# A gather-paced recommendation kernel: VectorE operations with two SBUF inputs replaced by operations that read PSUM

## The chip, the cores and the metric

One core of one Trainium2 chip. The metric is the device time of one launch, in microseconds. Several runs are made and their median is given. The cores of this chip have four compute engines that matter here: TensorE (matmuls, PE in the profile), VectorE (DVE), ScalarE (ACT) and GpSimd (POOL). GpSimd issues the indirect DMAs that gather rows of an embedding table.

## The reference, cut to what matters

For each of 16384 users, 69 rows of 96 floats are looked up (`u`), and one row for the label (`q`). A small net gives each looked-up row an attention weight, the weighted rows are summed in 10 groups, and a top net of three layers gives one number per user.

```python
u = emb[batch_user]                       # 16384 x 69 x 96
z = concat([q, u, q - u, q * u])
h = dice(z @ W1 + b1, a1)                 # dice(x) = (alpha*(1-p) + p)*x, p = sigmoid(x)
att = (h @ W2 + b2) @ W3 + b3
pre = where(batch_user < ITEM_NUM, u * att, 0)
pooled = einsum('gf,bfe->bge', window, pre)
x = concat([pooled, ql])
h = dice(bn(x @ Wf1 + bf1), af1)
h = dice(bn(h @ Wf2 + bf2), af2)
return h @ Wf3 + bf3
```

Here `ql` is the label's row, and `q` is that row repeated for each of the user's 69. An id equal to ITEM_NUM must give a zero row, although the table has a row of its own there.

## The kernel before: the parts that the change and the argument touch

The kernel works in 1104 steps. In each step GpSimd gathers 8 times 128 rows, one indirect DMA each, and TensorE turns the rows of that step, computes the hidden layer of an earlier one, and pools the rows of one that lies eight steps back. With 128 gathers for the labels there are 8960 gathers.

```python
def map_ids(n, ids):                      # ids that mean "no row" move to a zero row at the table's end
    rows = ipool.tile([P, NT], I32, tag="rows", name=f"rows{n}")
    nc.vector.scalar_tensor_tensor(rows, ids[:, 0:NT], float(ITEM_NUM), ids[:, 0:NT], ALU.is_ge, ALU.add)
    return rows
...
def gather(dst, index):                   # 128 rows, one index per partition
    nc.gpsimd.indirect_dma_start(out=dst, out_offset=None, in_=emb,
        in_offset=bass.IndirectOffsetOnAxis(ap=index, axis=0))
...
def hidden(i, ph, uT, quT):
    ...
    nc.vector.tensor_mul(y, ph, y)        # one input in PSUM, one in SBUF
...
def spread(b, row):                       # once in 4 steps
    pt = ps_x.tile([P, 4, 4, 32], F32, tag="x", name=f"patt{b}")
    for t in range(4):
        nc.tensor.transpose(pt[:, t]..., row[:, t * P : (t + 1) * P], ident)
    nc.vector.tensor_scalar(w, pt[:, :, :, 0:2]..., bb, None, ALU.add)
    nc.vector.tensor_tensor(rw..., R...to_broadcast(...), w...to_broadcast(...), ALU.mult)   # both in SBUF
    return rw
...
# top net, each half of the first layer (and the second layer likewise)
nc.vector.tensor_scalar(x1, p1, S_BN, sbf1[h], ALU.mult, ALU.add)
nc.scalar.activation(g1, x1, AF.Sigmoid, scale=S_DICE)
nc.scalar.activation(g1, g1, AF.Identity, bias=af1c[h], scale=naf1c[h])
nc.vector.tensor_mul(x1, x1, g1)          # both in SBUF
```

## Time and profile before

| | kernel before |
|---|---|
| time, unprofiled, first three runs | 11350.36 us (11344.71 to 11351.59) |
| span of the profiled execution | 13499.4 us |
| GpSimd busy / gathers | 8525.6 us / 8960 |
| TensorE busy, granted clock | 10109.4 us, 0.658 |
| VectorE busy | 3172.4 us |

The two times differ by 2149 us, and a reader has to decide which of them the profile explains. The prediction does that from the gathers, and shows the lines. A row of the groups reads: line, engine, operation, output <- inputs, shapes, count | busy us in all, mean ns of one | idle us just before it, and what ended that idle time.

### The profile page before, as it was taken

Reading aid. Unit: us, or ns where it says so; the run is one execution under the profiler, and the core shown is the slowest. Engines: PE = TensorE matmul, PEld = TensorE weight load, DVE = VectorE, ACT = ScalarE, POOL = GpSimd, SP = SyncE. Lnnn points to the kernel's source line nnn. Section 1 sums busy time; section 2 is a strip of 40 time slices with the busy share of each in tenths; the row PEclk is TensorE's granted clock in tenths of the full one; section 3 lists DMA queues with packets and bytes.
Section 4 is the critical chain, followed back from the end, with each engine's and each line's share of the span. In section 5 each row is a group of like instructions: output and inputs, shape, how many; then the busy total and the mean of one; then the engine's idle time right before and its main releaser. Section 6 shows DMA issues by size and latency. Waiting matters only on the chain.

```text
span 13499.4 us, 108113 instructions
## 1 busy us (share of the span) xinstructions
PE 10109.4 (75%) x41348; PEld 5068.4 (38%) x41348; DVE 3172.4 (24%) x5424; ACT 3740.6 (28%) x6086; POOL 8525.6 (63%) x8966
## 2 busy tenths in 40 slices
PE   4777777778777776777777777777778777787778
PEld 2333333334333333333333333333333333343334
DVE  2222222222222222222222222222222222222222
ACT  1222222223222222222222222222222222232222
POOL 6666666666666666666666666666666666666664
PEclk5666666666666677666666666766666666666657
DMA  1111111111111111111111111111111111111111
GB/s 37 34 34 35 33 34 33 34 35 34 34 34 34 34 34 33 33 34 34 33 34 34 34 34 35 34 33 33 33 35 34 34 33 34 35 34 33 34 32 22
DMA packets 295008, 453.59 MB, mean 34 GB/s; under 512 B 145952, under 2 KB 151104, under 8 KB 294496
## 3 DMA queue, kind: packets, MB, share of 16 engines
q0 software_dynamic: 286720, 440.98, 15.5%
q8 instruction: 331, 5.42, 0.2%
q1 hardware_dynamic: 6142, 4.77, 0.1%
q14 instruction: 181, 1.48, 0.0%
q10 hardware_dynamic: 1634, 0.94, 0.0%
HBM read 446.04 MB, written 0.07 MB: 33 GB/s over the span
## 4 chain that ended last, share of the span: by engine, by line
PE 62%; another core or an unknown queue 15%; issue 12%; ACT 5%; DVE 5%; POOL 1%; DMA 0%; DVEq 0%; POOLq 0%; ACTq 0%
PE ph L326 22%; PE acc L376 15%; PE ptr L308 9%; PE p L406 5%; PE prow L337 4%; PE ph L278 4%; DVE y L330 3%; ACT y L329 2%; PE patt L353 2%; ACT y L328 1%; PE pa L346 1%; DVE quT L311 1%; ACT uT L319 1%; POOL u L227 1%
## 5 line engine op out<-in xcount | busy, mean ns | idle before, releaser
L227 POOL DMA_INDIRECT u<-in_emb,rows x8832 | 8401.6, 951 | 4802.4 <-issue 2351.7
L376 PEld LDWEIGHTS acc<-rw,u 128*96 128x96 f32 x16384 | 2185.5, 230 | 2828.8 <-issue 2828.2
L278 PE MATMUL ph<-zrow 1*128 1x512 bf16 x1104 | 532.2, 482 | 2654.8 <-DVE y L330 1760.5
L319 ACT COPY uT<-ptr 96x512 f32<-96x512 f32 x2208 | 1285.2, 582 | 3713.4 <-DVE quT L311 2616.7
L376 PE MATMUL acc<-rw,u 128*96 128x20 f32 x16384 | 2298.9, 292 | 1.8 <-DVE rw L359 1.3
L308 PEld LDWEIGHTS ptr<-ident,u 128*96 128x96 f32 x8832 | 1312.6, 167 | 1912.8 <-issue 1547.8
L308 PE MATMUL ptr<-ident,u 128*96 128x128 f32 x8832 | 1785.7, 362 | 326.1 <-issue 247.9
L326 PE MATMUL ph<-uT,A 96*64 96x512 f32 x4416 | 1954.0, 955 | 27.4 <-issue 26.7
L326 PE MATMUL ph<-quT,w 96*64 96x512 f32 x4416 | 1915.7, 909 | 54.5 <-issue 53.2
L328 ACT ACTIVATE y<-ph 128x512 f32<-128x512 f32 x1104 | 659.4, 597 | 4602.9 <-remote 2107.1
L330 DVE TENSOR_TENSOR y<-ph,y 128x512 f32<-128x512 f32 x1104 | 763.7, 692 | 4689.6 <-ACT y L329 2396.5
L311 DVE TENSOR_TENSOR quT<-ptr,qT 96x512 f32<-96x512 f32 x2048 | 1340.0, 680 | 1866.9 <-remote 887.1
L385 DVE COPY pooled<-acc 96x160 f32<-96x160 f32 x1008 | 430.6, 427 | 2811.6 <-remote 1020.7
L326 PEld LDWEIGHTS ph<-quT,w 96*64 96x64 f32 x4416 | 491.4, 202 | 1279.1 <-issue 1277.6
L329 ACT ACTIVATE y<-y,a1c,na1c 128x512 f32<-128x512 f32 x1104 | 897.4, 813 | 37.2
L281 ACT COPY ph<-cT 128x512 f32<-128x512 f32 x1008 | 591.4, 587 | 281.5 <-remote 75.0
L406 PE MATMUL p<-pooled,wf 96*100 96x512 f32 x1280 | 620.0, 625 | 6.3 <-issue 4.8
L337 PE MATMUL prow<-y,v 128*32 128x512 f32 x2208 | 546.6, 932 | 79.7 <-issue 41.3
L326 PEld LDWEIGHTS ph<-uT,A 96*64 96x64 f32 x4416 | 307.0, 183 | 766.4 <-issue 696.0
L339 ACT COPY row<-prow 128x512 f32<-128x512 f32 x276 | 161.4, 585 | 864.0 <-remote 345.4
L353 PE MATMUL patt<-ident,row 128*128 128x128 f32 x1104 | 267.9, 386 | 113.4 <-DVE pre L347 88.1
L406 PEld LDWEIGHTS p<-pooled,wf 96*100 96x100 f32 x1280 | 219.7, 181 | 270.1 <-issue 267.3
(71 smaller groups left out, 2535.6 us busy)
## 6 DMA issues: line engine op xcount, KB each, us to landing
u<-in_emb,rows POOLq DMA_INDIRECT x8832
ids<-in_idx SPq DMA_DIRECT2D x32, 140.0 KB
q<-in_emb,ids POOLq DMA_INDIRECT x128
wf<-in_Wf ACTq DMA_DIRECT2D x1, 825.0 KB
out<-res SPq DMA_DIRECT2D x32, 2.0 KB
w<-in_W SPq DMA_DIRECT2D x1, 96.0 KB
wf<-in_Wf ACTq DMA_DIRECT2D x1, 62.5 KB
a1c<-in_a SPq DMA_DIRECT2D x2, 0.2 KB
```

Source lines behind the costliest of these rows:

```text
L227: nc.gpsimd.indirect_dma_start(out=dst, out_offset=None, in_=emb, in_offset=bass.IndirectOffsetOnAxis(ap=index, axis=0),)
L278: nc.tensor.matmul(ph, zrow[:, 0:P], zrow, start=True, stop=False)
L308: nc.tensor.transpose(ptr[:, t * P : (t + 1) * P], u[:, 4 * j + t, :], ident)
L311: nc.vector.tensor_tensor(quT[:, j, :].rearrange("e (s f) -> e s f", f=FM), ptr.rearrange("e (s f) -> e s f", f=FM), by_field(q[:, k * NS ...
L319: nc.scalar.copy(uT[:, j, :], ptr)
L326: nc.tensor.matmul(ph[j * H1 : (j + 1) * H1, :], w, x[:, j, :], start=False, stop=last)
L328: nc.scalar.activation(y, ph, AF.Sigmoid, scale=S_DICE)
L329: nc.scalar.activation(y, y, AF.Identity, bias=a1c, scale=na1c)
L330: nc.vector.tensor_mul(y, ph, y)
L337: nc.tensor.matmul(pr[32 * k : 32 * (k + 1), :], v2, y, start=True, stop=True)
L376: nc.tensor.matmul(pa[:, j, 2 * t : 2 * t + 2, :].rearrange("e n g -> e (n g)"), u[:, 4 * j + t, :], rw[:, i % 4, j, t, :], start=True, st ...
L406: nc.tensor.matmul(p1, w[:, h * DH : (h + 1) * DH], x, start=(k == 0), stop=(k == KTOP - 1))
```

## The change

The intent: no VectorE operation in the steady part of the kernel takes both inputs from SBUF, since in the first profile all 161 gathers that took over 0.975 us lie beside an operation with two; the prediction names the page that says why that may be. The spread takes the attention straight from the transposes' PSUM, the top net applies its gates to the PSUM sum, and the ids are no longer mapped: the gathers of users read a copy of the table whose last row is zero.

```diff
-        w = rpool.tile([P, 4, 2, 4], F32, tag="w", name=f"w{b}")
-        nc.vector.tensor_scalar(w, pt[:, :, :, 0:2]..., bb, None, ALU.add)
-        nc.vector.tensor_tensor(rw..., R..., w..., ALU.mult)
+        for j in range(2):
+            nc.vector.scalar_tensor_tensor(
+                rw[:, :, j, :],
+                pt.rearrange("p t k j -> p (t k) j")[:, :, j : j + 1].to_broadcast([P, 16, 2 * G]),
+                bb,
+                R.rearrange("p (o g) -> p o g", o=1).to_broadcast([P, 16, 2 * G]),
+                ALU.add, ALU.mult)
...
+    def dice(x, g, p, b, weights):
+        sb, sa, sna = weights
+        nc.scalar.activation(g, p, AF.Sigmoid, bias=sb, scale=S_BN * S_DICE)
+        nc.scalar.activation(g, g, AF.Identity, bias=sa, scale=sna)
+        nc.vector.scalar_tensor_tensor(x, p, b, g, ALU.add, ALU.mult)
...
-        nc.vector.tensor_scalar(x1, p1, S_BN, sbf1[h], ALU.mult, ALU.add)
-        nc.scalar.activation(g1, x1, AF.Sigmoid, scale=S_DICE)
-        nc.scalar.activation(g1, g1, AF.Identity, bias=af1c[h], scale=naf1c[h])
-        nc.vector.tensor_mul(x1, x1, g1)
+        dice(x1s[n][:, h, :], g1, p1, bf1c[h], dice1[h])
...
-                gather(u[:, 4 * j + t, :], rows[n][:, 4 * k + t : 4 * k + t + 1])
+                gather(rows, u[:, 4 * j + t, :], ids[n][:, 4 * k + t : 4 * k + t + 1])
...
-        "emb": np.concatenate([x["emb"], np.zeros((1, E), np.float32)], axis=0),
+        "emb": x["emb"],
+        "rows": np.concatenate([x["emb"][:ITEM_NUM], np.zeros((1, E), np.float32)], axis=0),
```

The 45 operations that build V from two SBUF inputs, in the first steps, stay.

## The prediction

> **What bounds the kernel now.** I read the table of engines first, then the costliest groups, then all gathers one by one in the timeline, then the last 130 us. The times in the profile are of a profiled execution of 13499 us; unprofiled the kernel takes 11350 us, so the first question is which of the two shows the true limit. The page says:
>
> ```profile
> PE 10109.4 (75%) x41348; PEld 5068.4 (38%) x41348; DVE 3172.4 (24%) x5424; ACT 3740.6 (28%) x6086; POOL 8525.6 (63%) x8966
> PE 62%; another core or an unknown queue 15%; issue 12%; ACT 5%; DVE 5%; POOL 1%; DMA 0%; DVEq 0%; POOLq 0%; ACTq 0%
> L227 POOL DMA_INDIRECT u<-in_emb,rows x8832 | 8401.6, 951 | 4802.4 <-issue 2351.7
> ```
>
> By the first two lines TensorE looks like the limit and GpSimd like a bystander: 63% busy, 1% of the chain of waits. That is the profiled execution, whose chain holds 27% of "unknown queue" and "issue". The third line tells the other story: 8832 gathers (with 128 for the labels 8960), 951 ns each, and idle ahead of them 2351.7 us put down to "issue", about 0.3 us a gather. The timeline shows it as a fixed gap:
>
> ```profile
> 6018.92 0.43 DVE L385 COPY pooled<-acc 96x160 f32<-96x160 f32 x1 [0.73 <-PE acc L376]
> 6019.16 0.95 POOL L227 DMA_INDIRECT u<-in_emb,rows  x1 [8.03 <-PE acc L376]
> 6019.56 0.25 DVE L356 TENSOR_SCALAR w<-patt,bb 128x32 f32<-128x32 f32 x1 [0.20 <-PE patt L353]
> 6019.84 0.82 DVE L359 TENSOR_TENSOR rw<-R,w 128x640 f32<-128x640 f32 x1
> 6020.41 1.08 POOL L227 DMA_INDIRECT u<-in_emb,rows  x1 [0.30 <-issue]
> 6021.79 0.95 POOL L227 DMA_INDIRECT u<-in_emb,rows  x1 [0.30 <-DMA u<-in_emb,rows]
> 6023.04 0.95 POOL L227 DMA_INDIRECT u<-in_emb,rows  x1 [0.30 <-issue]
> ```
>
> The reader is to see two things. The starts are 1.25 us apart (6021.79 to 6023.04): a gather costs 0.95 + 0.30 whatever else goes on. And the gather at 6020.41 takes 1.08 instead: the product rw with its two SBUF inputs had been running since 6019.84.
>
> Over the whole timeline, 7703 gathers that follow one another without a wait and have no two-SBUF-input VectorE operation beside them start 1.2508 us apart on average. Then 8960 x 1.2508 = 11207 us is the least that GpSimd needs. In the profiled execution the intervals above 1.3 us add 2160 us over that pace; 11207 + 2160 + 3 of start (first gather at 3.3) + 130 after the last gather = 13500, the span. The unprofiled run has only 11350 - 11207 - 3 = 140 us for everything else. I conclude that unprofiled the gathers run nearly back to back, that GpSimd sets the pace, and that most TensorE stalls belong to the profiled execution. Three runs within 7 us of each other fit an engine with a fixed pace.
>
> The last piece is the end:
>
> ```profile
> 13368.43 0.94 POOL L227 DMA_INDIRECT u<-in_emb,rows  x1 [0.30 <-issue]
> ...
> 13419.61 1.94 PE L308 MATMUL ptr<-ident,u 128*96 128x128 f32 x8
> ...
> 13497.22 0.23 SPq L432 DMA_DIRECT2D out<-res  x1
> ```
>
> The last gather starts at 13368, but TensorE is five steps behind it and turns the last rows only at 13419.6; from there to the output it is 78 us. If TensorE keeps up, unprofiled, the tail is some 80 us, and 140 - 80 = 60 us is left for stretched gathers and stalls. This is an estimate from those rows.
>
> **What the Trainium skill says.** "SBUF — State Buffer", section Who interferes with whom: GpSimd's only read and write port are VectorE's second pair, and a VectorE instruction with two SBUF inputs contends with a GpSimd instruction that reads SBUF; whichever starts second "fully blocks". It also reports that tensor_tensor did not stall plain DMA, because descriptor generation needs the write interface (marked there as inferred). "Perfetto Trace Analysis", section DMA Instruction — SWDGE (GPSIMD), says such instructions do not read a tensor. An indirect gather does have to fetch its 128 indices, and here the trace decides: of 8960 gathers 158 took over 0.98 us (up to 1.56), and 157 of these lie beside a VectorE operation with two SBUF inputs. Beside operations with one PSUM and one SBUF input (quT 680 ns, y 692 ns, pre 736 ns) and beside the PSUM copies none is stretched to speak of. So the lock acts, on the index read.
>
> "VectorE: DVE Perf Modes", section on the errata, gives an fp32 tensor_tensor as (N+151)/0.96 ns: 824 ns for N=640, and the trace has 828.
>
> **The change part by part.**
>
> ```profile
> L330 DVE TENSOR_TENSOR y<-ph,y 128x512 f32<-128x512 f32 x1104 | 763.7, 692 | 4689.6 <-ACT y L329 2396.5 <-issue 874.0 <-PE ptr L308 754.8
> L359 DVE TENSOR_TENSOR rw<-R,w 128x640 f32<-128x640 f32 x276 | 228.4, 828 | 9.5
> L356 DVE TENSOR_SCALAR w<-patt,bb 128x32 f32<-128x32 f32 x276 | 66.0, 239 | 184.5 <-remote 67.5 <-PE patt L353 58.0 <-PE ptr L308 25.0
> L413 DVE TENSOR_TENSOR x<-x,g 100x512 f32<-100x512 f32 x64 | 44.5, 695 | 98.8 <-ACT g L412 63.3 <-ACT g L411 27.8 <-issue 7.7
> L424 DVE TENSOR_TENSOR x<-x,g 80x512 f32<-80x512 f32 x32 | 22.0, 688 | 49.4 <-ACT g L423 26.3 <-ACT g L422 13.9 <-issue 9.3
> L108 DVE SCALAR_TENSOR_TENSOR rows<-ids 128x276 int32<-128x276 int32 x32 | 13.8, 432 | 0.6 <-DMA ids<-in_idx 0.6
> L222 DVE SCALAR_TENSOR_TENSOR V<-wf,wr,V 96x200 f32<-96x200 f32 x45 | 19.1, 424 | 1.6
> ```
>
> The removed culprits are rw (276), x·g (64 + 32) and rows (32); V (45, at the start) stays. Row by row, taking each gather's excess over 0.945 to 0.947 us beside each line, the timeline gives: rw 40 us, x·g 6 + 2, rows 2, V 0.4.
>
> *Size unprofiled, two ways.* (a) Scale: profiled, the gathers' own pace fills 11207/13499 = 83% of the span, unprofiled 98.7%, so 51 x 1.19 = 61 us. (b) Geometry: a gather is stretched only if it starts between about 0.05 and 0.7 us after rw starts (delays of 0.61 us at 0.10 after, 0.42 at 0.28, 0.15 at 0.55, none beyond 0.7). That is a triangle: 0.69²/2 over a period of 1.25 is 0.19 us for each rw at a random phase, 53 us for 276. For the 0.69-us products 0.56²/2/1.25 = 0.125 x 96 = 12, for the maps about 2. Sum 67 us. If TensorE follows the gathers closely, rw's phase isn't random but fixed by the landing rows, and the sum could lie anywhere from nearly nothing to 0.6 x 276 = 170; the budget of about 60 us caps it.
>
> *Spread.* Before 0.24 + 0.83 = 1.07 us of VectorE. After: two scalar_tensor_tensor of 320 elements. From pre (512 elements, 736 ns) and V (200, 424 ns) such an operation costs about 1 ns per element and 0.22 fixed, 0.54 us each, 1.08 together: nothing gained or lost in VectorE time. The transposed rows' PSUM buffer is held 0.8 us longer, of steps of about 10 us.
>
> *Top net.* The 747-ns evacuation and the 695-ns product become one operation of 0.74 us: 96 x 0.7 = 67 us of VectorE time, on an engine that is 24% busy, so no gain by itself. ScalarE now reads the sum from PSUM: 597 ns as for y, against 630. The only buffer of the top net's sums is held through both gates, 0.63 + 0.81 + 0.74 and gaps = 2.3 us instead of 0.8. In mid-kernel the next half comes a step later and does not notice. In the tail, the second half's first matmul starts 1.5 us later, but the second half's gate chain and that of the second layer are each 0.8 us shorter: zero in sum.
>
> *Zero row.* 32 x 0.43 us of VectorE and a step ahead of the first gathers go; the four label gathers (5 us) hid that at the start. Same number of gathers, same row length.
>
> Sum: GpSimd loses about 60 us of stretches, everything else about zero: 11350 - 58 = 11292 us.
>
> **The rivals.** (1) TensorE sets the pace unprofiled too, as in the profiled chain (62% of it), and that 11350 lies 1.3% above GpSimd's floor is chance. Then stretched gathers were hidden in slack and nothing changes: 11345 to 11355. For it: 9.2 us of TensorE per step against 10.15 of gathers, close at the low granted clock of 0.658. Against: the coincidence, and the tight runs. One chance in four. (2) The phase was fixed at a bad spot and the tail is shorter than 80 us: up to 90 us gained, 11260. (3) Stretches go, but the time is lost again as waits for the gathered-row buffers, since TensorE's margin is thin: some 20 to 40 us gained, 11310 to 11330. (4) The two PSUM-source operations are slower than estimated through their strided and repeated reads; even at 1 us each VectorE stays far below its limit, and rw is wanted only in the next step: no effect.
>
> **Range and chances.** Faster by over 2% would need 11123 us, below the 11207 that the gathers alone take, so it needs an unprofiled gather faster than 1.25 us with stretches above 200 us: 2%. Slower by 2% has no mechanism that I can see: 1%. Eight times in ten between 11250 and 11352; the upper end covers rival 1.
>
> **What would show it.** Right: in the new profile no gather beyond the first 10 steps takes over 1.0 us, the mean falls from 951 to 947 ns, the gap stays at 0.30; two 320-element operations near 0.54 us replace w and rw; VectorE busy falls by about 80 us (67 + 14). The profiled span itself may stay near 13500 since TensorE stalls set it, and proves little. Wrong: stretched gathers that remain (then not the second SBUF input), a shorter pace everywhere (then the pace had a part that I took as fixed), or vanished stretches with an unchanged time (then rival 1).

## The result, and the profile after

| | before | after |
|---|---|---|
| median of 6 runs | 11350.98 us | 11281.1 us |
| lowest to highest | 11344.71 to 11353.67 | 11277.29 to 11283.22 |
| ratio of fast runs | | 0.9938 (0.9926 to 0.9951) |

The ratio is the mean time of the changed kernel's fast runs over that of the other's in the same rounds, so it is not quite the ratio of the medians. The change gains 70 us, 0.6%: within 2%, and clear of noise.

The profiled execution of the changed kernel took 11280.6 us, as long as the unprofiled ones. Its engines, its chain of waits and its gathers, from the page:

```profile
PE 9823.7 (87%) x41348; PEld 4777.1 (42%) x41348; DVE 3089.8 (27%) x5299; ACT 3767.8 (33%) x6086; POOL 8464.1 (75%) x8966
POOL 37%; PE 32%; issue 17%; DMA 11%; ACT 2%; DVE 1%; POOLq 0%
L223 POOL DMA_INDIRECT u<-in_rows,ids x8832 | 8342.3, 945 | 2690.8 <-issue 2433.4
```

The chain now runs through GpSimd's gathers (37% of the span against 1% in the first profile) and their landing (DMA 11%). "Another core or an unknown queue" is gone. The mean gather takes 945 ns instead of 951, and the idle time before the 8832 gathers, 2690.8 us, is the fixed 0.30 us each and nothing else. A piece of the timeline with a spread in it:

```profile
5032.66 0.94 POOL L223 DMA_INDIRECT u<-in_rows,ids  x1 [0.31 <-issue]
...
5033.91 0.95 POOL L223 DMA_INDIRECT u<-in_rows,ids  x1 [0.30 <-issue]
5033.96 1.01 DVE L352 SCALAR_TENSOR_TENSOR rw<-patt,bb,R 128x320 f32<-128x320 f32 x2
...
5035.16 0.95 POOL L223 DMA_INDIRECT u<-in_rows,ids  x1 [0.30 <-issue]
...
5036.41 0.94 POOL L223 DMA_INDIRECT u<-in_rows,ids  x1 [0.31 <-PE ptr L304]
```

The gathers start 1.25 us apart straight past the spread. In this piece none starts within the spread; in the whole profile 159 start within one of its operations (from 0.06 us after the operation's start to 0.16 us before its end), and none of them is stretched, where in the first profile 116 of 116 beside `rw` were. Listing all 8960 in the timeline, I find not one wait beyond the fixed gap. Their spacing is 1.2490 us where unstretched, and 17 are stretched (over 0.975 us), by 1.9 us in all; these lie in the first 127 us, beside the operations on V, save for the very first gather. The new and the remaining operations, from the groups of VectorE and of ScalarE:

```profile
L352 DVE SCALAR_TENSOR_TENSOR rw<-patt,bb,R 128x320 f32<-128x320 f32 x552 | 277.8, 545 | 78.7 <-PE patt L349 73.3
L395 DVE SCALAR_TENSOR_TENSOR x<-p,bf1c,g 100x512 f32<-100x512 f32 x64 | 48.0, 750 | 284.9 <-ACT g L394 284.9
L218 DVE SCALAR_TENSOR_TENSOR V<-wf,wr,V 96x200 f32<-96x200 f32 x45 | 19.0, 423 | 1.6
```

```profile
L324 ACT ACTIVATE y<-ph 128x512 f32<-128x512 f32 x1104 | 659.6, 597 | 3894.0 <-PE ph L322 3893.7
L393 ACT ACTIVATE g<-p,dice 100x512 f32<-100x512 f32 x64 | 44.0, 687 | 158.6 <-PE p L408 158.6
```

The two spread operations take 545 ns each and overlap by some 0.08 us, so that VectorE is busy for 277.8 us over the 276 spreads, 1.01 us each, where the pair before took 228.4 + 66.0 = 294.4 us, 1.07 each. VectorE gained 17 us there, spread over the whole kernel; e9 below shows that VectorE's time is not what counts.

The end of the timeline, from the last gather to the output:

```profile
11195.32 0.95 POOL L223 DMA_INDIRECT u<-in_rows,ids  x1 [0.30 <-issue]
...
11278.37 0.23 SPq L428 DMA_DIRECT2D out<-res  x1
```

The whole span adds up: 3.4 us before the first gather, 8959 x 1.2490 = 11189.8, 1.9 of stretches and 85.3 from the last gather to the end make 11280.4 of 11280.6.

### The profile page after: what moved, and what is told of

Same layout as the page of the kernel before. It is cut to its first block, busy times and chain, and to the rows that moved or that the text cites. A ratio compares the mean times of both kernels' runs of the same rounds, so it can differ in the third digit from the quotient of the medians.

```text
span 11280.6 us, 108907 instructions
## 1 busy us (share of the span) xinstructions
PE 9823.7 (87%) x41348; PEld 4777.1 (42%) x41348; DVE 3089.8 (27%) x5299; ACT 3767.8 (33%) x6086; POOL 8464.1 (75%) x8966
## 4 chain that ended last, share of the span: by engine, by line
POOL 37%; PE 32%; issue 17%; DMA 11%; ACT 2%; DVE 1%; POOLq 0%
POOL u L223 36%; DMA u<-in_rows,ids 11%; PE ph L322 11%; PE acc L371 8%; PE p L408 4%; PE ptr L304 3%; PE prow L333 2%; PE ph L274 2%; POOL q L223 1%; ACT y L325 1%; PE pa L342 1%; PE patt L349 1%; DVE y L326 1%; ACT y L324 1%; PE pc L263 0%
## 5 line engine op out<-in xcount | busy, mean ns | idle before, releaser
L223 POOL DMA_INDIRECT u<-in_rows,ids x8832 | 8342.3, 945 | 2690.8 <-issue 2433.4
L304 PE MATMUL ptr<-ident,u 128*96 128x128 f32 x8832 | 2049.5, 356 | 1235.6 <-DMA u<-in_rows,ids 1215.8
L304 PEld LDWEIGHTS ptr<-ident,u 128*96 128x96 f32 x8832 | 1236.0, 156 | 3163.3 <-DMA u<-in_rows,ids 1585.8
L371 PEld LDWEIGHTS acc<-rw,u 128*96 128x96 f32 x16384 | 2073.1, 220 | 522.8 <-issue 521.1
L371 PE MATMUL acc<-rw,u 128*96 128x20 f32 x16384 | 2185.4, 284 | 1.2 <-DVE rw L352 0.6
L322 PE MATMUL ph<-uT,A 96*64 96x512 f32 x4416 | 1817.6, 916 | 0.0
L322 PE MATMUL ph<-quT,w 96*64 96x512 f32 x4416 | 1710.5, 866 | 0.0
L322 PEld LDWEIGHTS ph<-quT,w 96*64 96x64 f32 x4416 | 449.1, 196 | 1092.4 <-issue 1092.4
L333 PE MATMUL prow<-y,v 128*32 128x512 f32 x2208 | 452.0, 905 | 0.0
L408 PE MATMUL p<-pre,V 96*100 96x512 f32 x640 | 310.7, 618 | 0.0
```

What stands on the lines that cost most here:

```text
L223: nc.gpsimd.indirect_dma_start(out=dst, out_offset=None, in_=table, in_offset=bass.IndirectOffsetOnAxis(ap=index, axis=0),)
L304: nc.tensor.transpose(ptr[:, t * P : (t + 1) * P], u[:, 4 * j + t, :], ident)
L322: nc.tensor.matmul(ph[j * H1 : (j + 1) * H1, :], w, x[:, j, :], start=False, stop=last)
L333: nc.tensor.matmul(pr[32 * k : 32 * (k + 1), :], v2, y, start=True, stop=True)
L371: nc.tensor.matmul(pa[:, j, 2 * t : 2 * t + 2, :].rearrange("e n g -> e (n g)"), u[:, 4 * j + t, :], rw[:, 4 * t + i % 4, j, :], start=Tru ...
L408: nc.tensor.matmul(p1, w[:, h * DH : (h + 1) * DH], x, start=(k == 0), stop=(k == KTOP - 1))
```

## The experiments

The lock theory: the gain is the stretched gathers, because a gather's index read waits for a VectorE operation with two SBUF inputs that started before it. The rivals: TensorE sets the pace, so that stretches lie in slack (rival 1); VectorE's time itself; and, from the first comparison, a pace theory. In the first profile of the kernel before the unstretched gathers are 1.2507 us apart, in the changed kernel 1.2490; times 8960 that would be 15 of the 70 us.

In the numbers below, "stretches" are the sum of each gather's time over 0.945 us, for gathers over 0.975 us, read gather by gather from the timeline and put to the operation with two SBUF inputs that overlaps it (to the earlier one where two do).

**The two states.** The chips used gave two kinds of times, for every kernel alike and unprofiled too: about 11.3 ms (the chip of e7 to e9, and that of the result), or 13.4 to 13.6 ms (the chips of e1 to e4, of e5 and e6, and of e10 to e12). I call them the fast and the stalled state. They are not told apart by the label that a run carries, since each chip was consistent in itself. All comparisons are within one call, on one chip. Each chip on record was used in one call only, so the record can't tell whether the chip or the moment makes the state. The changed kernel itself was never run in the stalled state, nor the kernel before profiled in the fast one. The granted TensorE clock differs between the states as well, 0.66 to 0.68 in the stalled one and 0.70 in the fast one, with the two kernels alike in each (0.701 and 0.702 on e7's chip): it is no rival for the 70 us. Whether it is a cause of the stalls or follows from them is not shown.

### e1: the kernel before again

No edit.

> The kernel before, unchanged, for a profile without the TensorE stalls of the first one. Lock theory: span near 11350 us, gathers back to back as in the changed kernel, stretched ones only beside operations with two SBUF inputs, their excess 55 to 70 us in all. Pace theory (unstretched gathers of the kernel before are 1.2508 us apart against 1.2490 in the changed one, and that is 16 of the 70 us): the unstretched pace is 1.2508 here too. If it is 1.2490, the pace was a matter of the disturbed first profile and the stretches must make up all of the 70 us. TensorE theory (rival 1): gathers with waits of 1 us and more between them.

Measured: 13422.55 us (14 runs), in the stalled state, as the kernel before beside it (13423.76). So times near the first profile's 13499 us come in runs without a profile too. The page's engines, chain and gathers:

```profile
PE 10004.8 (75%) x41348; PEld 4983.6 (37%) x41348; DVE 3169.1 (24%) x5424; ACT 3746.5 (28%) x6086; POOL 8546.5 (64%) x8966
PE 61%; another core or an unknown queue 17%; issue 10%; ACT 5%; DVE 5%; POOL 2%; DMA 0%; DVEq 0%; POOLq 0%; ACTq 0%
L227 POOL DMA_INDIRECT u<-in_emb,rows x8832 | 8423.2, 954 | 4718.0 <-issue 2209.9
```

The idle time before the gathers, 4718 us, is some 2000 us above the fixed gaps: GpSimd waits for row buffers that TensorE frees late. In this state rival 1 is right. Still all 189 stretched gathers lie beside an operation with two SBUF inputs (rw 58.6 us, the top net's products 10.0, maps 1.9, V 0.5; 71.0 in all). The unstretched pace was 1.2508.

### e2, e6, e11: the spread alone put back

The edit in short:

```diff
-        (two scalar_tensor_tensor from PSUM)
+        w  = pt + bb          # tensor_scalar, PSUM -> SBUF
+        rw = R * w            # tensor_tensor, both inputs in SBUF
```

> The changed kernel with the spread by w and rw (two SBUF inputs) put back, 276 products of 828 ns. Lock theory: 11281 + 53 at a random phase = 11334, 11320 to 11340 if the spread's share is that of the first profile (40 of 52); its gathers over 1.0 us lie only beside rw. If VectorE or TensorE time were what the change gained, this run would stay near 11281, since both forms need 1.07 us of VectorE.

> The changed kernel with only the spread by w and rw put back, in the same state. Lock theory at 11350 us for the kernel before: rw has most of the stretches, so 11281 + 40 to 55 from stretches, and if the slower unstretched pace of e2 (1.2508 against 1.2490) comes with it another 16: 11321 to 11352. If VectorE time were the cause: 11281.

> The changed kernel with only the spread by w and rw put back, in the fast state. Lock theory: 11273 to 11281 + 40 to 50 of stretches + up to 16 from the slower unstretched pace that e2 and e6 showed (1.2508): 11315 to 11345. VectorE-time rival: 11273 to 11281.

All three fell in the stalled state, so the expected times could not be tested. Measured: 13452.15, 13575.65 and 13452.45 us, against the kernel before at 13423.76, 13547.36 and 13433.45 (ratios 1.0018, 1.0026 and 1.0014). Stretches in the trace: rw 44.2, 45.4 and 50.1 us, V 0.6 to 0.7, and 0.2 us at the very first gather. This part alone brings back most of the stretches of the kernel before.

### e3, e12: the top net alone put back

The edit in short:

```diff
-        dice(x1s[n][:, h, :], g1, p1, bf1c[h], dice1[h])
+        x1 = S_BN * p1 + sbf1          # tensor_scalar, PSUM -> SBUF
+        g1 = gates(x1)                 # ScalarE
+        x1 = x1 * g1                   # tensor_tensor, both inputs in SBUF
```

> The changed kernel with the top net's evacuation and product in SBUF put back (96 products of 690 ns with two SBUF inputs). Lock theory: 8 to 14 us more, 11289 to 11295. If the shorter gate chain mattered by itself, the tail after the last gather would change from 85 us by over 2 us.

> The changed kernel with only the top net's evacuation and product in SBUF put back, in the fast state. Lock theory: stretches 8 to 14 us more; the unstretched pace of e3 was 1.2482 against 1.2490, which takes back 7 us: in sum 11275 to 11290, tail within 2 us of 85.

Measured, stalled state: 13377.58 us (ratio 0.996 to the kernel before) and 13386.05 us (0.9966). Stretches by the top net's products: 8.1 and 14.4 us, the 8 to 14 that was expected. The time in the fast state stays untested.

### e4: the maps of the ids alone put back

The edit in short:

```diff
+        rows = ids + (ids >= ITEM_NUM)     # scalar_tensor_tensor, both inputs in SBUF, 32 times
-        gather(rows_table, u, ids)
+        gather(emb_with_zero_row, u, rows)
```

> The changed kernel with the maps of the ids put back (32 operations of 432 ns with two SBUF inputs, one table for all gathers). Lock theory: 1 to 4 us more, 11282 to 11285. Pace theory: if the table or the index tile sets the pace of an unstretched gather, up to 16 us more, 11297, with the mean unstretched pace at 1.2508 us.

Measured, stalled state: 13400.3 us (ratio 0.9976). Stretches by the maps: 3.8 us.

The parts together: rw 44 to 50, top net 8 to 14, maps 4, that is 56 to 68 us of stretches. The kernel before shows 50.3, 71.0, 55.9 and 68.4 in its four profiles. The stretches thus agree with the sum of the three parts, and in those four profiles rw has 38.5, 58.6, 42.3 and 54.7 us of them, 76% to 83%.

On the clock, the stalled state follows the stretches poorly. With the spread put back (45 to 51 us of stretches) the kernel is 0.1 to 0.3% slower than the kernel before, which has 50 to 71. With the spread left in its new form it is 0.2 to 0.4% faster. Where TensorE is the limit, the stretches are not what sets the time; what makes the 0.2 to 0.4% there is open.

### e5, e10: the kernel before, for a profile in the fast state

No edit.

> The kernel before once more, for a profile in the state that takes 11350 us (the first profile and the chip of e1 to e4 were in one that takes 13400 to 13500 us, unprofiled too). Lock theory, if it is the 11350 us state: no wait over 0.05 us between gathers beyond the fixed gap of 0.305, pace of the unstretched 1.2508, so 8959 x 1.2508 + 3.4 + a tail of 83 to 88 = 11293 to 11297, and stretches of 54 to 58 us make up the rest to 11350. Rival 1 (TensorE sets the pace): waits of 1 us and more between gathers. If the chip is again in the 13400 us state, it repeats e1.

> The kernel before, third try for a profile in the state that takes 11340 to 11350 us (e7 to e9 were in it). Lock theory: gathers back to back with no waits, unstretched pace 1.2508 us, 8959 x 1.2508 + 3.4 + tail 83 to 88 = 11293 to 11297, the rest up to 11343 to 11350 is stretches, 48 to 58 us, beside operations with two SBUF inputs only. Rival 1: waits of 1 us and more between gathers.

Both fell in the stalled state: 13534.89 and 13415.23 us. Neither gives the profile that was wanted. A profile of the kernel before in the fast state therefore is missing from this study. But e10 bears on the pace theory: its unstretched gathers are 1.2482 us apart, and e1's, the same kernel, 1.2508. The changed kernel has 1.2490 in its first profile and 1.2483 in e7. Its variants e2, e4, e6 and e12 have 1.2504 to 1.2508, e3 and e11 1.2481 to 1.2482. Both paces come with parts of the change in or out, so the change alone does not set the pace. Within one profile the pace is constant. What remains open is which pace the kernel before had in the fast runs. If it was 1.2507 there, the pace would make 8959 x 0.0017 to 0.0024 = 15 to 22 of the 70 us and the stretches the rest; if it was 1.2483, the stretches would make about all. The stretches of the four stalled profiles, 50 to 71 us, fit either.

### e7: the changed kernel again

No edit.

> The changed kernel, unchanged, beside the kernel before on the same chip. In the 11350 us state: 11281. In the 13400 us state, where TensorE is the limit (about 2000 us of waits between gathers in e1 and e5): rival 1 holds there, the stretches lie in slack and the two kernels are the same within 0.5% (e3 and e4, which lack nearly all of the stretches or only a part, were 0.4% and 0.2% faster than the kernel before).

Measured, fast state: 11273.17 us (3 runs, 11270.39 to 11273.92) against 11343.02 of the kernel before (15 runs), ratio 0.9938. The result repeats in another call: 69.9 us between the medians. Its gathers come again with no wait and 1.9 us of stretches: 3.4 + 8959 x 1.2483 + 1.9 + 82.8 after the last gather is 11271.6, and its span is 11271.4.

### e8: one more product in each step, both inputs in SBUF

```diff
         nc.vector.tensor_mul(y, ph, y)
+        nc.vector.tensor_mul(spare[:, 1, :], y, spare[:, 0, :])
```

> The changed kernel with one more VectorE product in each of the 1104 steps, 128x512, both inputs in SBUF (result unused). Lock theory: each such 0.69 us product stretches a gather that starts 0.05 to 0.56 us after it, 0.125 us each on average at a random phase: 115 to 140 us of stretches in the trace in either state (50 to 350 if the phase is not random), none of them before the product's start, and in the 11281 us state the same on the clock, 11330 to 11600. Rival (VectorE time itself): the PSUM control gives the same.

### e9: the control, one of its inputs in PSUM

```diff
         nc.vector.tensor_mul(y, ph, y)
+        nc.vector.tensor_mul(spare[:, 1, :], ph, spare[:, 0, :])
```

> The control: the same added products, same shape and time, but the first input is the PSUM sum ph instead of y in SBUF. Lock theory: stretches stay at the 2 us of the changed kernel (the 45 operations on V) and the time at 11281 in the fast state, within 0.1%; in the other state within 0.5% of the kernel before. If added VectorE time is what costs, it moves as much as the two-SBUF dose.

Measured on one chip with e7, fast state:

| | time (us) | against e7 | VectorE busy (us) | stretches (us) | after the last gather (us) |
|---|---|---|---|---|---|
| e7 changed kernel | 11273.17 | | 3091.7 | 1.9 | 82.8 |
| e8 both inputs in SBUF | 11370.72 | +97.6 | 3836.1 | 98.1 | 80.1 |
| e9 one input in PSUM | 11277.60 | +4.4 | 3718.2 | 1.6 | 86.8 |

The added groups of e8 and e9 first, then their gathers:

```profile
L329 DVE TENSOR_TENSOR spare<-y,spare 128x512 f32<-128x512 f32 x1104 | 765.4, 693 | 37.6
...
L225 POOL DMA_INDIRECT u<-in_rows,ids x8832 | 8432.0, 955 | 2691.2 <-issue 2336.7
```

```profile
L329 DVE TENSOR_TENSOR spare<-ph,spare 128x512 f32<-128x512 f32 x1104 | 751.6, 681 | 0.0
...
L225 POOL DMA_INDIRECT u<-in_rows,ids x8832 | 8334.9, 944 | 2691.7 <-issue 2358.2
```

The operations have the same shape and nearly the same length, 693 and 681 ns. Only the one with two SBUF inputs makes the mean gather 11 ns longer. In the timeline of e8 one such meeting looks like this:

```profile
5009.42 0.69 DVE L329 TENSOR_TENSOR spare<-y,spare 128x512 f32<-128x512 f32 x1
5009.85 1.07 POOL L225 DMA_INDIRECT u<-in_rows,ids  x1 [0.30 <-issue]
...
5011.23 0.94 POOL L225 DMA_INDIRECT u<-in_rows,ids  x1 [0.30 <-issue]
...
5017.96 0.69 DVE L329 TENSOR_TENSOR spare<-y,spare 128x512 f32<-128x512 f32 x1
...
5018.72 0.94 POOL L225 DMA_INDIRECT u<-in_rows,ids  x1 [0.30 <-issue]
```

A gather that starts 0.43 us after the product is 0.13 us longer. One that starts 0.76 us after the next product, when that has ended, is not. The same meeting in the control e9, with a gather 0.34 us after the product:

```profile
5014.20 0.68 DVE L329 TENSOR_TENSOR spare<-ph,spare 128x512 f32<-128x512 f32 x1
5014.54 0.94 POOL L225 DMA_INDIRECT u<-in_rows,ids  x1 [0.30 <-issue]
```

By the table below a gather at that distance would be some 0.2 us longer in e8; here it takes its usual 0.94. Over the products of e8 the stretch falls in a straight line with the distance from the product's start to the next gather's start:

| the gather starts after the product by | products | mean stretch of that gather |
|---|---|---|
| 0.1 to 0.2 us | 60 | 0.41 us |
| 0.2 to 0.3 | 48 | 0.31 |
| 0.3 to 0.4 | 111 | 0.22 |
| 0.4 to 0.5 | 131 | 0.11 |
| 0.5 to 0.6 | 106 | 0.02 |
| 0.6 to 1.3 | 580 | 0.00 |

The line ends at 0.56 us, and a finer count shows why. A held gather ends 0.82 us after the product's end, whenever it started (0.811 to 0.825 us). That is 0.13 us less than its usual 0.945, so it loses the time from 0.13 us after its start to the product's end, and 0.69 - 0.13 = 0.56. The other edge: of 132 gathers that start between 0.13 us before the product and 0.04 us after it none is stretched, although most of each runs beside the product; of the 37 that start 0.04 to 0.1 us after it 35 are. So the one that comes second waits. Counted the same way as for the spread, 412 of 416 gathers that start within an added product are stretched in e8, and none of 390 in e9. What the gather waits for no trace shows; that it is the read of the index is my inference.

What follows: stretches cost time one for one in the fast state, 98.1 - 1.9 = 96.2 us in the trace against 97.6 on the clock. VectorE time does not: the control adds 627 us of VectorE time and 4.4 us to the kernel, of which 4.0 lie after the last gather. The sum in e8 is below the 115 to 140 us expected, 0.087 us for each product instead of 0.125: the estimate left out that gathers within 0.05 us of the product's start go free (with that edge it is 0.51² / 2 / 1.25 = 0.104), and the gathers don't meet the products at a random phase (48 to 131 in steps of 0.1 us, by the table).

## Why the prediction was right, point by point

- **The bound.** Right for the state that it was made for. The changed kernel's profile shows GpSimd without a single wait, and its span is the sum of gathers, start and tail. The reason given for the 2149 us between profile and run failed: the prediction said that "most TensorE stalls belong to the profiled execution". e1, e5 and e10 show the same stalls, with unprofiled runs of 13350 to 13590 us beside them. They belong to a state in which whole calls fell. The sentence that the profiled span "may stay near 13500" was wrong for the same reason: it came to 11281.
- **The floor of 11207 us.** Too high by 16 to 22 us for the changed kernel, whose pace was 1.2490 and 1.2483 in the two fast profiles. If the kernel before had that pace too in its fast runs, which no profile shows, the budget of 60 us for stretches was too small by as much.
- **The stretches, about 60 us.** The right mechanism: stretched gathers went, and e8 and e9 show in the fast state that stretches cost time and that two SBUF inputs make them. That it is the index read that is held stays an inference. The size was off somewhat: the measured gain is 70 us in both comparisons, 12 more than the 58 forecast. The first profile's 50 us was the lowest of four (50.3, 71.0, 55.9, 68.4, mean 61.4, of which V's 0.5 stays). The prediction's own scaling, from 83% to 98.7% occupation, makes 72 us of that mean. Its geometry, 67 us, was nearer than the budget that capped it, but by luck: its triangles leave out the edge of 0.05 us that it had itself read. With it they give 0.65² / 2 / 1.25 = 0.17 x 276 and 0.10 x 96, with the maps' 2 in all 59 us. A slip without effect: 0.6 x 276 is 166, not 170. How far the 12 us are stretches, the pace of the kernel before or its tail stays open without its fast profile. How much of the 70 us each part has in the fast state was not run; by the stalled traces the spread has about four fifths.
- **No stretches left beyond the first ten steps.** Nearly right: the last three lie at 124 to 126 us, in the twelfth step, beside the last operations on V. There are none after that.
- **VectorE.** 0.54 us for a spread operation: 0.545. 0.74 for the gated sum: 0.75. About 80 us of VectorE time less: 3172.4 - 3089.8 = 82.6. The sum fits because two things offset each other: the spread lost 17 us, where the prediction had nothing since it did not see that the two operations overlap, and operations that were not changed were busy some 14 us longer (9 of them on `quT`). VectorE's time is worth nothing by itself, as e9 shows from the other side.
- **ScalarE and the tail.** The sigmoid from PSUM was put at 597 ns and takes 687 with its bias, 0.09 us in each gate chain; the tail was put at some 80 us and is 85.3 and 82.8. Too small to matter.
- **The rivals.** TensorE as the limit (1): true in the stalled state, false in the fast one, where no gather waits. A worse phase with up to 90 us gained (2): the actual 70 lies between it and the forecast. Waits for row buffers in place of the stretches (3): none. Slow PSUM reads (4): none.

What stays open: the profile of the kernel before in the fast state, for which three tries found the other state, and with it the exact split of the 70 us; the share of each part of the change on the clock; and what stalls TensorE in the stalled state.

## What to carry to other kernels

When a kernel is paced by GpSimd's indirect gathers, look for gathers that take longer than their mode and at what VectorE runs beside them: in e8 an operation with both inputs in SBUF held gathers that started after it and before its end, while in e9 the same operation with one input in PSUM held none and cost 4.4 us in 11273. Size the gain before the work: here 404 such operations cost at most 0.6% of the time, and the 0.95 + 0.30 us of each gather, which stays, costs 99%. Before trusting a profile's bound, hold its span against the unprofiled time, and if they differ, find the engine whose own pace explains the shorter one.

## What the Trainium skill lacked or had wrong

- "SBUF — State Buffer", section Who interferes with whom: it has the rule that a VectorE instruction with two SBUF inputs contends with a GpSimd instruction that reads SBUF, and says that tensor_tensor did not stall DMA. It lacks that an indirect gather counts as such a reader: 420 gathers were stretched by 96.4 us beside the added products of e8, none beside those of the control. It also lacks where the edge lies: gathers that started up to 0.04 us after the product's recorded start were not held (132 of 132 in e8), later ones ended 0.82 us after the product's end.
- "Perfetto Trace Analysis", section DMA Instruction — SWDGE (GPSIMD): these instructions "do not read a tensor". For the indirect gather the stretches in e8 speak against that, though no trace shows the read itself. The page's section GPSIMD Engine Instruction advises to time GpSimd by the spacing of starts, not by the reported duration. Here the two agree: 0.944 us and the gap of 0.305 make the spacing of 1.249.
- "DMA: Bandwidth & Descriptors" gives no issue cost for an indirect gather. Here it is 0.944 us busy and a gap of 0.305 for 128 rows of 384 bytes, and the spacing varies between executions of one kernel, from 1.2482 (e10) to 1.2508 us (e1).
- "VectorE: DVE Perf Modes", section on the errata, gives tensor_tensor to 0.5% (824 ns for 640 elements, 828 measured) but has no row for scalar_tensor_tensor from PSUM: 545 ns for 320 elements, 750 for 512.
- The same section's table, ScalarE from PSUM to SBUF, gives (172+512)/1.2 = 570 ns. The sigmoid without a bias takes 597, the one with a bias column 687. The two were not told apart by a run of their own.
- No page that I read has the stalled state: the same kernel takes 11343 us on one chip and 13424 on another, with 105 gaps of over 7 us between the starts of TensorE's weight loads and other non-matmul instructions in e1 (1461 us in all) against one, at the start, in the changed kernel's fast profile.
